# Merging one of four weight blocks partly on TensorE, and reordering the two-layer expert block around it

## The chip, the cores and the metric

One core of one Trainium2 chip runs the whole kernel. The metric is device time in microseconds for one execution, as the median of several runs. Besides these, one execution was recorded by the hardware profiler; its trace gives the start and the length of every instruction on every engine: TensorE (PE in the profile; its weight loads are PEld), VectorE (DVE), ScalarE (ACT), GpSimd (POOL) and SyncE's transfer queue (SP).

## The reference

The program is one layer of a graph network on 1250 nodes with 512 features: a two-step graph convolution, a linear-attention mixer, and at the end a feed-forward block whose weights are mixed at run time out of eight experts. The change touches only that last block:

```python
gh  = relu(x @ gfc1_w.T + gfc1_b)
g   = (gh @ gfc2_w.T + gfc2_b).mean(over the nodes)   # eight gates
W1m = W1 + sum_e g[e] * tv_W1[e]                      # 256 x 512
b1m = b1 + g @ tv_b1
W2m = W2 + sum_e g[e] * tv_W2[e]                      # 512 x 256
b2m = b2 + g @ tv_b2
h   = relu(x @ W1m.T + b1m)
out = h @ W2m.T + b2m
y   = layernorm(x + out) * ln_g' + ln_b'
```

The gates are means over all nodes, so no merged weight exists before the whole gating layer is done. Here `x` is the layer-normed input of the block; the result is added to the residual stream. All data are float32.

## The kernel before

**Layout.** A tile is 128 nodes: ten node tiles (`NT`), the last with 98 rows. Features lie in `DT = 4` blocks of 128. The first layer has 256 outputs, `FT = 2` blocks of 128. `xn2_t` holds the normed input with the features on the partitions; `CHUNKS` cuts its 1250 columns into three pieces (418, 416, 416), so that one piece fits a PSUM bank.

**Order.** From the last graph convolution on, every engine's order is the order in which the Python code issues the instructions (`last_order`, a manual schedule); semaphores are put in wherever data, or the reuse of a buffer, ask for it. The eight PSUM banks are handed out at first use, the one that came free longest ago first.

**The stretch in question**, from L1274 to the end of `usual_block`:

1. `gate_products` (L1278, L1281) computes the eight gates, once as a row on every partition (`pg`) and once as a column (`pg9`). DVE turns the first into `gate` (L1297), ACT the second into `gate9` (L1298).
2. The merged first-layer weights `m1` have four feature blocks of 128 x 256, and each is summed over eight experts in one of two ways. On DVE: a chain of `scalar_tensor_tensor` into a PSUM accumulator (`merge`, L1312), and at its end, unless `alone`, an addition of the base weights (L1315). On ACT and POOL: ACT scales the expert's block in place (`scaled`, L1307) and POOL adds it to `m1` (L1347 for block 3, L1320 in `merge_far`). Before the change DVE sums block 0 (`alone`), then 1, then 2, and ACT with POOL sums block 3.
3. The second-layer weights `m2` have two halves of 128 x 512: ACT with POOL sum half 1 (`merge_far`), DVE sums half 0.
4. `joined(c)` (L1325) multiplies block `c` of `m1` with block `c` of the input into six open PSUM banks (`parts`: two output blocks by three pieces). After `c = 3` ACT writes `a_t` with bias and ReLU (L1328).
5. The merged second bias comes from one product with `gate9` (L1334); ACT copies it to `b2` (L1342) and back to PSUM (L1358). It is added to the normed input of tiles 0 to 4 by DVE (L1364) and of tiles 5 to 9 by POOL (L1366).
6. The output loop: `out_product(t)` (L1374) are two products over 512 columns; `out_sum` (L1378) and `out_gauge` (L586, L588, L590) follow on DVE and ACT. Then tiles 2, 5 and 9 are finished by DVE (`out_near`, L1392 to L1395) and the other seven by ACT and POOL (`out_far`, L1402 to L1408; two POOL operations, L1406 and L1407).

The matrix unit takes one float32 product of this program as two LDWEIGHTS and two MATMUL instructions: the 24 products of `joined` are 48 rows in the profile.

Of the kernel before, what the change touches and what calls it, by code (L numbers as in the profile page):

```python
# [9 lines left out]
F32 = mybir.dt.float32  # L10
# [3 lines left out]
AF = mybir.ActivationFunctionType  # L14
ALU = mybir.AluOpType
AX = mybir.AxisListType

P = 128
N = 1250
D = 512  # L20
DT = D // P
NT = 10
FF = 256
FT = FF // P
NE = 8
# [16 lines left out]
CHUNKS = [(0, 418), (418, 416), (834, 416)]  # L42


def rows(t):
    return min(P, N - t * P)
# [479 lines left out]
def usual_block(  # L526
# [23 lines left out]
    nc = tc.nc  # L550
# [3 lines left out]
    tmp = ctx.enter_context(tc.tile_pool(name="tmp", bufs=2))  # L554
# [7 lines left out]
    def bank(dtype=F32):  # L562
        return psum.tile([P, 512], dtype, tag="bank", name="bank")
# [14 lines left out]
    ident = const.tile([P, P], F32, name="ident")  # L578
# [49 lines left out]
    def v(name, i=0, n=1):  # L628
        at = _COLS[name][0] + i
        return v_sb[:, at:at + n]  # L630
# [43 lines left out]
    g2bc = const.tile([NE, 1], F32, name="g2bc")  # L674
# [108 lines left out]
    key = e_d  # L783
# [333 lines left out]
    late = ctx.enter_context(tc.tile_pool(name="late", bufs=1, side="right"))  # L1117
    r9 = late.tile([NE + 1, 3, D], F32, name="r9")
    nc.sync.dma_start(out=r9, in_=rows9)
    m1 = late.tile([P, DT, FF], F32, name="m1")  # L1120
    nc.sync.dma_start(out=m1, in_=f_w1.rearrange("(c p) f -> p c f", p=P))
    m2 = late.tile([P, FT, D], F32, name="m2")
    nc.sync.dma_start(out=m2, in_=f_w2.rearrange("(c p) f -> p c f", p=P))
    t1s, t2s = [], []
# [11 lines left out]
    gate9 = late.tile([NE + 1, P], F32, name="gate9")  # L1136
# [137 lines left out]
    pg, pg9 = bank(), bank()  # L1274
# [20 lines left out]
    gate_products([DT - 1])  # L1295
    gate = late.tile([P, NE], F32, name="gate")
    nc.vector.scalar_tensor_tensor(gate, pg[:, 0:NE], 1.0 / N, v("g2b", 0, NE), op0=ALU.mult, op1=ALU.add)  # L1297
    nc.scalar.activation(gate9[0:NE, :], pg9[0:NE, 0:P], AF.Identity, bias=g2bc, scale=1.0 / N)  # L1298

    a_t = more.tile([P, FT, N], F32, tag="E", name="a_t")
    parts = [(f, b, bank()) for f in range(FT) for b in range(len(CHUNKS))]
    sums = [bank(), bank()]

    def scaled(dst, e, src):
        nc.scalar.activation(dst, src, AF.Copy, scale=gate[:, e:e + 1])  # L1307

    def merge(acc, dst, srcs, at, alone=False):

        for e in range(0 if alone else 1, NE):
            nc.vector.scalar_tensor_tensor(dst[at] if alone and e == NE - 1 else acc, srcs[e][at], gate[:, e:e + 1],  # L1312
                                           dst[at] if alone and e == 0 else acc, op0=ALU.mult, op1=ALU.add)
        if not alone:
            nc.vector.tensor_tensor(dst[at], acc, dst[at], ALU.add)  # L1315

    def merge_far(dst, srcs, at):
        for e in range(NE):
            scaled(srcs[e][at], e, srcs[e][at])
            nc.gpsimd.tensor_tensor(dst[at], dst[at], srcs[e][at], ALU.add)  # L1320

    def joined(c):
        for f, b, ps in parts:
            c0, cn = CHUNKS[b]
            nc.tensor.matmul(ps[:, :cn], m1[:, c, f * P:(f + 1) * P], xn2_t[:, c, c0:c0 + cn],  # L1325
                             start=(c == 0), stop=(c == DT - 1))
            if c == DT - 1:
                nc.scalar.activation(a_t[:, f, c0:c0 + cn], ps[:, :cn], AF.Relu, bias=mb1[:, f:f + 1])  # L1328

    def first(c):  # L1330
        return (slice(None), c, slice(None))


    nc.tensor.matmul(sums[1], gate9, r9[:, 0, :], start=True, stop=True)  # L1334
    b2 = late.tile([P, D], F32, name="b2")
    merge(sums[0][:, 0:FF], m1, t1s, first(0), alone=True)
    mb = late.tile([P, FT, NE], F32, name="mb")
    nc.gpsimd.tensor_tensor(mb, v("tvb1", 0, FT * NE).rearrange("p (f e) -> p f e", f=FT),
                            gate.unsqueeze(1).to_broadcast([P, FT, NE]), ALU.mult)
    mb1 = late.tile([P, FT], F32, name="mb1")  # L1340
    scaled(t1s[0][first(3)], 0, t1s[0][first(3)])
    nc.scalar.copy(b2, sums[1])  # L1342
    scaled(sums[1][:, 0:FF], 0, t1s[0][first(1)])
    for e in range(NE):
        if e:
            scaled(t1s[e][first(3)], e, t1s[e][first(3)])
        nc.gpsimd.tensor_tensor(m1[first(3)], m1[first(3)], t1s[e][first(3)], ALU.add)  # L1347
    joined(0)
    scaled(sums[0][:, 0:FF], 0, t1s[0][first(2)])
    merge(sums[1][:, 0:FF], m1, t1s, first(1))  # L1350
    joined(1)
    merge_far(m2, t2s, first(1))
    scaled(sums[1], 0, t2s[0][first(0)])
    merge(sums[0][:, 0:FF], m1, t1s, first(2))
    joined(2)
    nc.vector.tensor_reduce(mb1, mb, AX.X, ALU.add)
    nc.gpsimd.tensor_tensor(mb1, mb1, v("fb1", 0, FT), ALU.add)
    nc.scalar.copy(sums[0], b2)  # L1358
    merge(sums[1], m2, t2s, first(0))
    joined(3)  # L1360
    for t in range(NT):
        n = rows(t)
        if t < NT // 2:
            nc.vector.tensor_tensor(xn2[0:n, t, :], xn2[0:n, t, :], sums[0][:n], ALU.add)  # L1364
        else:
            nc.gpsimd.tensor_tensor(xn2[0:n, t, :], xn2[0:n, t, :], b2[:n], ALU.add)  # L1366

    last = {}

    def out_product(t):  # L1370
        n = rows(t)
        last[t] = bank()
        for f in range(FT):
            nc.tensor.matmul(last[t][:n], a_t[:, f, t * P:t * P + n], m2[:, f, :], start=(f == 0), stop=(f == FT - 1))  # L1374

    def out_sum(t):
        n = rows(t)
        nc.vector.tensor_tensor(last[t][:n], last[t][:n], xn2[0:n, t, :], ALU.add)  # L1378

    def out_gauge(t):  # L1380
        last[t] = (last[t],) + spread(last[t][:rows(t)], rows(t))
# [26 lines left out]
        nc.sync.dma_start(out=out[t * P:t * P + n, :], in_=m[:n])  # L1408

    for t in range(NT + 1):  # L1410
        if t < NT:
            out_product(t)
            out_sum(t)
        if t >= 1:
            (out_near if t - 1 in (2, 5, 9) else out_far)(t - 1)
        if t < NT:
            out_gauge(t)
# [5 lines left out]
def graph_block(tc, *args):  # L1423

    unusual = usual_block(tc, *args)
    with tc.If(unusual > 0):
        general_block(tc, *args)
# [58 lines left out]
```

## Time and profile before

| What | us |
|---|---|
| Median of three runs (574.11 to 574.74) | 574.61 |
| The profiled execution, its own time | 574.88 |
| Its span, from the first to the last instruction | 572.9 |
| Busy PE / DVE / ACT / POOL in the span | 546.3 / 324.8 / 242.0 / 80.1 |
| `gate` done (L1297, start 517.44) | 517.61 |
| First product of `joined` starts (L1325) | 521.91 |
| First `out_product` starts (L1374) | 541.42 |
| First POOL operation of the output loop (L1406) | 547.16 |
| Last POOL operation starts (L1407) | 565.97 |

How to read it: times within the trace count from the start of the span. The execution's own time is 1.98 us more than its span. A row of a view gives a start, a length, an engine, a source line and the tile names "out<-in"; "idle before" is how long the engine had stood still and who released it. PEclk is the TensorE clock that was granted in a stretch, as a share of full speed.

### The profile page before, as it was taken

What the parts mean: (1) busy time and instruction counts of PE and PEld (TensorE: products, weight loads), DVE (VectorE), ACT (ScalarE), POOL (GpSimd) and SP (SyncE); (2) the same over time, 40 slices, a digit from 0 to 9 for tenths busy, and PEclk for the clock granted to TensorE, in tenths of its full rate; (3) what the DMA queues carried; (4) which work ended last, traced back from release to release, by engine and by line L of the source; (5) the groups of instructions that cost most, each with busy time, mean ns of one, the idle gap of its engine ahead of it and who ended that gap; (6) DMA issues with size and microseconds to landing.
All of it is one profiled execution on the core that took longest, in us unless ns stands there. A gap on an engine that the chain in (4) does not pass through costs nothing.

```text
span 572.9 us, 6957 instructions
## 1 busy us (share of the span) xinstructions
PE 546.3 (95%) x2367; PEld 369.1 (64%) x2367; DVE 324.8 (57%) x1097; ACT 242.0 (42%) x533; POOL 80.1 (14%) x77
## 2 busy tenths in 40 slices
PE   8799999999999999999999999999999999997990
PEld 7665568799955477777854454459995557764540
DVE  4579999976899734444425534111113248708693
ACT  5676664454444112322333443113323456727242
POOL 7200000000000000000013331000000001106975
PEclk9899999999999999999999999999999999997995
DMA  9400200020030020000311002000009120402023
GB/s 287 176 1 1 74 2 1 1 74 2 1 113 36 0 74 0 1 1 1 111 37 52 22 1 73 0 0 1 2 0 348 55 74 1 146 1 75 0 76 110
DMA packets 19285, 29.10 MB, mean 51 GB/s; under 512 B 1529, under 2 KB 8185, under 8 KB 19240
## 3 DMA queue, kind: packets, MB, share of 16 engines
q1 hardware_dynamic: 18984, 28.32, 14.6%
q8 instruction: 20, 0.33, 0.2%
q10 hardware_dynamic: 256, 0.25, 0.2%
q14 instruction: 25, 0.20, 0.1%
HBM read 26.01 MB, written 2.56 MB: 50 GB/s over the span
## 4 chain that ended last, share of the span: by engine, by line
PE 87%; DVE 5%; ACT 3%; POOL 2%; issue 1%; DMA 1%; POOLq 0%; DVEq 0%; ACTq 0%
PE bank L576 28%; PE bank L981 16%; PE bank L968 12%; PE bank L917 6%; PE bank L1037 6%; PE bank L849 5%; PE bank L1064 5%; PE bank L1325 3%; PE bank L606 2%; PE bank L1374 1%; POOL m L1406 1%; POOL m L1407 1%; DVE st L586 1%; PE bank L902 1%; ACT xn L600 1%
## 5 line engine op out<-in xcount | busy, mean ns | idle before, releaser
L981 PE MATMUL bank<-adj,y_h 128*128 128x416 f32 (+1 forms) x240 | 86.5, 361 | 1.1 <-DVE adj L851 1.1
L981 PE MATMUL bank<-adj,y_l 128*128 128x416 f32 (+1 forms) x240 | 84.4, 352 | 0.0
L834 DVE TENSOR_SCALAR oh_k<-count,e_d 128x240 f16<-128x240 f16 x324 | 82.6, 274 | 0.0
L1083 POOL TENSOR_TENSOR m<-m,ls_bc 128x512 f32<-128x512 f32 (+1 forms) x10 | 12.7, 1269 | 447.3 <-ACT m L600 447.3
L968 PE MATMUL bank<-w,h_t 128*128 128x512 f32 (+1 forms) x160 | 70.4, 592 | 0.0
L576 PE MATMUL bank<-z_t,w 128*128 128x416 f32 (+1 forms) x192 | 68.9, 513 | 0.0
L576 PEld LDWEIGHTS bank<-z_t,w 128*128 128x128 f32 x192 | 36.1, 189 | 31.8 <-issue 29.9
L832 DVE TENSOR_SCALAR oh_s<-count,s_lo 128x128 f16<-128x128 f16 x220 | 54.1, 246 | 0.0
L968 PEld LDWEIGHTS bank<-w,h_t 128*128 128x128 f32 (+1 forms) x160 | 29.4, 188 | 34.8 <-issue 34.5
L614 DVE SCALAR_TENSOR_TENSOR z_t<-u,m_sb,z_t 128x416 f32<-128x416 f32 (+1 forms) x24 | 15.7, 653 | 59.8 <-ACT u L613 59.8
L981 PEld LDWEIGHTS bank<-adj,y_h 128*128 128x128 f32 x240 | 45.1, 188 | 2.6 <-issue 2.1
L981 PEld LDWEIGHTS bank<-adj,y_l 128*128 128x128 f32 x240 | 45.2, 188 | 1.2 <-issue 0.7
L849 PE MATMUL bank<-oh_k,oh_s 128*128 128x240 f16 x324 | 41.4, 266 | 1.4 <-ACT oh_s L818 1.2
L849 PEld LDWEIGHTS <-oh_s 128*128 128x128 f16 x324 | 31.6, 98 | 15.8 <-issue 5.1
L612 ACT ACTIVATE z_t<-bank,v_sb 128x416 f32<-128x416 f32 (+1 forms) x24 | 14.6, 608 | 61.5 <-PE bank L981 61.5
L851 DVE TENSOR_TENSOR adj<-adj,bank 128x240 f32 x81 | 32.3, 399 | 13.9 <-PE bank L849 12.5
L995 DVE BATCH_NORM_STATS2 bst<-bank 128x6 f32<-128x416 f32 (+1 forms) x24 | 14.4, 600 | 42.9 <-ACT h_t L994 42.9
L917 PE MATMUL bank<-kk,xn 128*128 128x128 f32 (+1 forms) x320 | 38.4, 275 | 0.0
L576 PE MATMUL bank<-xn_t,lw 128*128 128x256 f32 (+2 forms) x128 | 37.6, 439 | 0.3 <-ACT xn_t L607 0.3
L917 PEld LDWEIGHTS bank<-kk,xn 128*128 128x128 f32 (+1 forms) x320 | 37.0, 192 | 0.1
L1064 PE MATMUL bank<-mixer,q_t 128*128 128x512 f32 (+1 forms) x80 | 36.3, 592 | 0.0
L576 PE MATMUL bank<-xn_t,gw 128*128 128x256 f32 (+2 forms) x128 | 35.3, 427 | 0.9 <-ACT xn_t L607 0.9
(166 smaller groups left out, 800.0 us busy)
## 6 DMA issues: line engine op xcount, KB each, us to landing
t<-in_tv_w SPq DMA_DIRECT2D x12, 512.0 KB, 7.5
w<-in_conv_w SPq DMA_DIRECT2D x4, 1024.0 KB, 5.5
x_in<-in_x SPq DMA_DIRECT2D x9, 256.0 KB, 4.6
xt<-in_x SPq DMA_DIRECT2D x9, 256.0 KB, 4.1
out<-m SPq DMA_DIRECT2D x9, 256.0 KB, 2.4
rest<-in_tv_w SPq DMA_DIRECT2D x4, 512.0 KB, 4.8
lw<-in_lin_w SPq DMA_DIRECT2D x4, 256.0 KB, 4.9
wk<-in_w_qkv SPq DMA_DIRECT2D x1, 1024.0 KB, 7.0
```

What stands on the lines that cost most here:

```text
L576: nc.tensor.matmul(ps[:, :cn], lhs(c), rhs(c), start=(c == 0), stop=(c == k - 1))
L614: nc.vector.scalar_tensor_tensor(dst, u[:, :cn], minus(*slope), dst, op0=ALU.mult, op1=ALU.add)
L832: nc.vector.tensor_scalar(oh_s[:, j, :], count16[:, 0:P], s_lo[:, b, j:j + 1], None, op0=ALU.is_equal)
L834: nc.vector.tensor_scalar(oh_k[:, j, :], count16, key[:, b, j:j + 1], None, op0=ALU.is_equal)
L849: nc.tensor.matmul(ps[:, 0:NT * W], oh_s[:, j, :], oh_k[:, j, :], start=(j == 0), stop=(j == J - 1))
L851: nc.vector.tensor_tensor(adj_r[:, :, at], adj[:, :, at], ps[:, 0:NT * W].rearrange("p (s d) -> p s d", s=NT), ALU.add)
L917: nc.tensor.matmul(ps[:, c * P:(c + 1) * P], xn[0:n, t, c * P:(c + 1) * P], k_nodes(f)[0:n, t, :], start=(t == 0), stop=(t == NT - 1))
L968: nc.tensor.matmul(ps[:n], h_t[:, c, t * P:t * P + n], w1[:, c, :], start=(c == 0), stop=(c == DT - 1))
L981: nc.tensor.matmul(ps[:, :cn], y[0:n, s, f * P:(f + 1) * P], adj_r[0:n, s, c0:c0 + cn], start=(s == 0 and y is ys[0]), stop=(s == NT - 1 a ...
L1037: nc.tensor.matmul(ps[:n], xn_t[:, c, t * P:t * P + n], wq[:, c, :], start=(c == 0), stop=(c == DT - 1))
L1064: nc.tensor.matmul(ps[:n], q_t[:, h, t * P:t * P + n], mixer[:, h, :], start=(h == 0), stop=(h == DT - 1))
L1325: nc.tensor.matmul(ps[:, :cn], m1[:, c, f * P:(f + 1) * P], xn2_t[:, c, c0:c0 + cn], start=(c == 0), stop=(c == DT - 1))
```

## The change

Block 0 of `m1` is cut in two column halves. The left half (columns 0 to 127, output block `f = 0`) is summed by TensorE: eight 128 x 128 identities, each scaled by one gate (`gated`; four made by DVE, four by ACT), and a plain identity for the base weights are multiplied with the weights into one PSUM bank, and ACT copies the sum into `m1`. The right half stays on DVE. Block 1 moves from DVE to ACT and POOL. Blocks 2 and 3 are summed together by DVE in one chain of 512 columns, in place of two chains of 256. The product for the second bias moves from ahead of `joined(0)` to behind it, into the bank of DVE's accumulator, so that the copy back to PSUM goes; the copy to `b2` then stands in ACT's order ahead of the scaling for `m2`. The scaling and adding for half 1 of `m2` is issued in two groups of four, with the start value of half 0 between them. `parts` is ordered by piece first, and the two products of `joined(3)` that belong to the last piece are issued behind two output tiles.

```diff
-    nc.scalar.activation(gate9[0:NE, :], pg9[0:NE, 0:P], AF.Identity, bias=g2bc, scale=1.0 / N)
-    parts = [(f, b, bank()) for f in range(FT) for b in range(len(CHUNKS))]
+    parts = [(f, b, bank()) for b in range(len(CHUNKS)) for f in range(FT)]
     sums = [bank(), bank()]
...
+    def flat(w, c0, c1):
+        return w[:, c0:c1, :].rearrange("p c f -> p (c f)")
...
+    def merge_far(dst, srcs, es):
+        for e in es:
+            scaled(srcs[e], e, srcs[e])
+            nc.gpsimd.tensor_tensor(dst, dst, srcs[e], ALU.add)
+    def joined(c, which):
+        for f, b, ps in which:
...
+    gated = [tmp.tile([P, 2, P], F32, tag="xt", bufs=4, name="gated") for _ in range(NE // 2)]
+    one = [flat(t, 1, 2) for t in t1s]
+    two = [flat(t, 2, 4) for t in t1s]
+    for e in (0, 1, 4, 5):
+        nc.vector.tensor_scalar(gated[e // 2][:, e % 2, :], ident, gate[:, e:e + 1], None, op0=ALU.mult)
+    scaled(gated[1][:, 0, :], 2, ident)
+    scaled(gated[1][:, 1, :], 3, ident)
+    nc.scalar.activation(gate9[0:NE, :], pg9[0:NE, 0:P], AF.Identity, bias=g2bc, scale=1.0 / N)
+    merge_far(flat(m1, 1, 2), one, [0])
+    scaled(gated[3][:, 0, :], 6, ident)
+    scaled(gated[3][:, 1, :], 7, ident)
+    nc.tensor.matmul(sums[1][:, 0:P], ident, m1[:, 0, 0:P], start=True, stop=False)
     for e in range(NE):
+        nc.tensor.matmul(sums[1][:, 0:P], gated[e // 2][:, e % 2, :], t1s[e][:, 0, 0:P],
+                         start=False, stop=(e == NE - 1))
+    acc = sums[0][:, 0:FF - P]
+    for e in range(NE):
+        nc.vector.scalar_tensor_tensor(m1[:, 0, P:FF] if e == NE - 1 else acc, t1s[e][:, 0, P:FF], gate[:, e:e + 1],
+                                       m1[:, 0, P:FF] if e == 0 else acc, op0=ALU.mult, op1=ALU.add)
+    merge_far(flat(m1, 1, 2), one, [1])
+    nc.scalar.copy(m1[:, 0, 0:P], sums[1][:, 0:P])
+    joined(0, sorted(parts, key=lambda p: p[0]))
+    merge_far(flat(m1, 1, 2), one, [2])
+    scaled(sums[1], 0, two[0])
+    merge_far(flat(m1, 1, 2), one, range(3, NE))
     nc.vector.tensor_reduce(mb1, mb, AX.X, ALU.add)
+    merge(sums[1], flat(m1, 2, 4), two)
     nc.gpsimd.tensor_tensor(mb1, mb1, v("fb1", 0, FT), ALU.add)
+    nc.tensor.matmul(sums[0], gate9, r9[:, 0, :], start=True, stop=True)
+    nc.scalar.copy(b2, sums[0])
...
+    far2 = [t[:, 1, :] for t in t2s]
+    joined(1, parts)
+    merge_far(m2[:, 1, :], far2, range(4))
+    shifted(0)
+    scaled(sums[1], 0, t2s[0][:, 0, :])
+    merge(sums[1], m2[:, 0, :], [t[:, 0, :] for t in t2s])
+    merge_far(m2[:, 1, :], far2, range(4, NE))
+    joined(2, parts)
+    joined(3, parts[0:4])
+    for t in range(1, NT):
+        shifted(t)
...
     for t in range(NT + 1):
+        if t == 2:
+            joined(3, parts[4:])
```

`shifted(t)` is the addition of item 5 for one tile, unchanged.

More of the change, by code (lines that the diff above doesn't have):

```diff
@@ L1307, in scaled, with merge @@
         nc.scalar.activation(dst, src, AF.Copy, scale=gate[:, e:e + 1])
[L1309 to L1323, printed above, removed]
+    def flat(w, c0, c1):
+        return w[:, c0:c1, :].rearrange("p c f -> p (c f)")
+    def merge(acc, dst, srcs):
+        for e in range(1, NE):
+            nc.vector.scalar_tensor_tensor(acc, srcs[e], gate[:, e:e + 1], acc, op0=ALU.mult, op1=ALU.add)
+        nc.vector.tensor_tensor(dst, acc, dst, ALU.add)
+    def merge_far(dst, srcs, es):
[4 more added lines that the diff above has]
+        for f, b, ps in which:
             c0, cn = CHUNKS[b]
@@ L1328, in joined @@
                 nc.scalar.activation(a_t[:, f, c0:c0 + cn], ps[:, :cn], AF.Relu, bias=mb1[:, f:f + 1])
[L1330 to L1336, printed above, removed]
     mb = late.tile([P, FT, NE], F32, name="mb")
@@ L1340, in usual_block @@
     mb1 = late.tile([P, FT], F32, name="mb1")
-    scaled(t1s[0][first(3)], 0, t1s[0][first(3)])
-    nc.scalar.copy(b2, sums[1])
-    scaled(sums[1][:, 0:FF], 0, t1s[0][first(1)])
-    for e in range(NE):
[L1345 to L1352, printed above, removed]
@@ L1353, in usual_block @@
-    scaled(sums[1], 0, t2s[0][first(0)])
-    merge(sums[0][:, 0:FF], m1, t1s, first(2))
-    joined(2)
+    b2 = late.tile([P, D], F32, name="b2")
+    gated = [tmp.tile([P, 2, P], F32, tag="xt", bufs=4, name="gated") for _ in range(NE // 2)]
[4 more added lines that the diff above has]
+    scaled(gated[1][:, 0, :], 2, ident)
@@ L1356, in usual_block, with shifted @@
     nc.vector.tensor_reduce(mb1, mb, AX.X, ALU.add)
+    merge(sums[1], flat(m1, 2, 4), two)
     nc.gpsimd.tensor_tensor(mb1, mb1, v("fb1", 0, FT), ALU.add)
[L1358 to L1361, printed above, removed]
+    nc.tensor.matmul(sums[0], gate9, r9[:, 0, :], start=True, stop=True)
+    nc.scalar.copy(b2, sums[0])
+    def shifted(t):
         n = rows(t)
```

## The prediction

> **What bounds the kernel now.** I read the chain of waits first, since the change touches only the last 55 us:
>
> ```profile
> 517.44 0.18 DVE gate L1297
> ...
> 517.64 0.56 DVE bank L1312
> ...
> 521.37 0.49 DVE m L1312
> 521.86 0.04 issue
> 521.91 19.68 PE bank L1325 x48
> 541.59 6.88 PE bank L1374 x16
> ...
> 553.44 1.28 POOL m L1406
> ...
> 566.43 0.80 POOL m L1407
> ```
>
> After the gates the end waits for DVE's eight steps on block 0 (4.2 us), then TensorE without a break up to the fourth output tile, then the output loop on DVE, ACT and POOL. Only what comes before the output loop, or makes TensorE quicker, can move the end.
>
> Second, windows of 3.41 us, with PE's busy time as the first number after the length and PEclk behind the five engines:
>
> ```profile
> 22.03:25.44 3.41, 0.97 (x6) 0.68 (x5) 2.19 (x8) 1.43 (x4) 0.00 (x0) 1.00 0.00 0
> 25.44:28.86 3.42, 3.42 (x12) 2.74 (x11) 1.60 (x6) 2.52 (x7) 0.00 (x0) 0.50 0.00 0
> ...
> 45.92:49.34 3.42, 2.22 (x14) 1.37 (x12) 3.42 (x18) 2.80 (x7) 0.00 (x0) 1.00 0.00 0
> 49.34:52.75 3.41, 3.41 (x15) 2.22 (x15) 3.17 (x15) 1.86 (x5) 0.00 (x0) 1.00 0.00 0
> ...
> 516.96:520.38 3.42, 1.87 (x8) 0.69 (x6) 2.73 (x7) 1.78 (x5) 0.94 (x2) 1.00 0.85 304
> 520.38:523.79 3.41, 1.88 (x3) 1.17 (x4) 3.23 (x7) 3.41 (x10) 2.58 (x4) 0.50 0.02 5
> 523.79:527.21 3.42, 3.42 (x6) 1.61 (x6) 3.21 (x8) 3.42 (x6) 3.19 (x5) 0.50 0.00 0
> ```
>
> Windows with 0.97, 1.87 and 1.88 us of PE work are followed by one at half clock; the one with 2.22 is not. So the wait for block 0 costs twice: TensorE stands still, and then runs at half clock until 527.2. The weight loads of L1325 stand 0.35 us apart at full clock and 0.70 before: 48 x 0.352 = 16.9, measured 19.7, so 2.8 us are lost.
>
> Third, the timeline of POOL, for what else must be ready:
>
> ```profile
> 526.50 2.62 POOL L1320 TENSOR_TENSOR m<-m,t 128x512 f32<-128x512 f32 x2
> 537.32 6.18 POOL L1366 TENSOR_TENSOR xn<-xn,b 128x512 f32<-128x512 f32 x5
> 547.16 1.26 POOL L1406 TENSOR_TENSOR m<-m,ln_g 128x512 f32<-128x512 f32 x1 [3.67 <-ACT m L600]
> ```
>
> Half 1 of `m2` takes POOL 10.7 us (526.50 to 537.20, 1.34 an addition), the five tiles 6.2; then POOL waits 3.7 us. Last, the groups that give prices:
>
> ```profile
> L917 PE MATMUL bank<-kk,xn 128*128 128x128 f32 (+1 forms) x320 | 38.4, 275 | 0.0
> L1312 DVE SCALAR_TENSOR_TENSOR bank<-t,gate,bank 128x256 f32<-128x256 f32 x20 | 9.8, 489 | 0.6
> L1307 ACT ACTIVATE t<-t,gate 128x256 f32<-128x256 f32 x8 | 3.4, 493 | 0.0
> L1347 POOL TENSOR_TENSOR m<-m,t 128x256 f32<-128x256 f32 x8 | 5.8, 728 | 2.8 <-ACT t L1307 2.4
> ```
>
> **The change part by part.** Times are on the axis of this trace; `gate` is done at 517.61.
>
> *Eight gated identities.* A DVE `tensor_scalar` of 128 f32 columns is not in the trace. Nearest: L785, 328 ns for 324 f32 columns, and L832, 246 ns for 128 f16 columns, started 0.17 apart. I take 0.23 and 0.15 apart (bounds 0.17 and 0.39 apart): DVE has its four by 518.3. ACT, from 493 ns (256 columns) and 708 (512): 0.385 each, 0.31 apart. ACT's order is identities 2 and 3, `gate9`, the first scaling of block 1, identities 6 and 7: done at 518.0, 518.35, 518.65, 519.05, 519.35, 519.66.
>
> *Nine narrow products.* They go into a bank long free (banks go out at first use, oldest free first), so the plain identity needs nothing and runs at 517.6. L917, which also accumulates with new weights each time, gives 0.12 an instruction, 0.24 a product. Isolated, the last pair of L1278 took 0.39 (517.01 to its end); that is the upper bound of a link. Back to back, seven products end at 519.4; the last two wait for ACT: 519.4 and 519.7; the sum is there at 520.2, ACT's copy (0.36, as L1298) at 520.6. `joined(0)` starts at 520.7 on the left half: **1.2 us earlier**. The right half costs DVE eight steps of 0.385 from 518.3 (128 columns, between 167 ns for 8 in L1297 and 489 for 256): 521.4, before its first product at 522.8. Experts 6 and 7 are read by TensorE from 519.4; SP issued those transfers before 466. No transfer is moved; the last pair (issued 515.78) has landed by 520 and is read after 529.
>
> [...]
>
> *The clock.* In 516.96 to 520.38 PE now has the gate products and some 2.4 us of chain, over 2.2 in sum, so it should stay at full speed: **2.8 us won**. [...] The four executions known lie between 574.11 and 574.88, so I keep the trace's 2.8.
>
> *Bias product behind `joined(0)`.* Before it ran in TensorE's idle time; now it is on the path: 2 x 0.433 = **0.87 lost**. `joined(0)` is done at 520.7 + 6 x 0.704 = 524.9, the product at 525.8.
>
> *Block 1 on ACT and POOL.* The first two additions end at 520.85. Behind ACT's copy (which waits for the chain) stand the third scaling, DVE's start value and the rest; from the fourth POOL adds without a break, 522.0 + 5 x 0.745 = 525.7. `joined(1)` needs it at 525.8: **nothing, without any slack**. A microsecond of delay on POOL is one on TensorE.
>
> *Blocks 2 and 3 on DVE.* Start value at 521.5, seven steps of 0.78 and one of 0.7: 527.8. `joined(2)` needs it at 530.0: nothing.
>
> *The copy to `b2` ahead of the scaling for `m2`.* ACT waits for the bias product until 526.0; behind it stand the eight scalings, so POOL begins half 1 at 527.35 instead of 526.50: 8 x 1.34 = 10.7, done at 538.05. `joined(3)` without its last pair ends at 525.8 + 16 x 0.704 = 537.05, the first product of tile 0 at 537.9; its second waits until 538.1: **0.15 lost**. DVE's half 0 is ready at 535.9 (ACT gives its start value at 529.7, behind four scalings), the tiles' additions at 538.3: covered by `out_sum(0)` at 539.1. Gone is the copy back to PSUM (0.59 of ACT, idle anyway).
>
> *Two products behind two tiles.* Tiles 0 and 1 come 1.4 us earlier than they would; tile 2 ends at the same TensorE work: 538.97 + 1.73 + 1.41 + 1.73 = 543.85. DVE sums tile 2 at 544.0; before, 546.77: 2.8 earlier. From there both loops are alike: DVE sets tile 3, for which POOL waited at 553.44. POOL's own work allows it: half 1 at 538.05, five tiles 544.3, tiles 0 and 1 by 549.5, tile 3 at 550.6. ACT's two `a_t` operations (1.3) stand ahead of tile 1's normalisation and move it to 545.9; POOL takes tile 1 at 546.9.
>
> *Sum:* -1.2 - 2.8 + 0.87 + 0.15 = -3.0; laid out with the waits, -2.8. 574.88 - 2.8 = 572.1; the median lies 0.27 below the profiled execution, which would give 571.8. I say **572.0**.
>
> **The rivals.**
>
> *One window at half clock (G).* If the chain counts for less than its busy time, the window from 520.38 is at half: 1.6 us lost, **573.6**. For: short products with waits between. Against: 2.22 us was enough at 45.92.
>
> *Two windows, as before (N).* Then `joined(0)` and the bias product end near 529, POOL starts half 1 at 530, and 3.3 of the gain are gone: **575.3**. This is also the case that the change doesn't do what it says. Against: from 520.7 TensorE has work, so 520.38 to 523.79 is busy.
>
> *The sum goes link by link (S), slower.* If each link waits for its own weights at 0.45, the sum ends at 521.6, `joined(0)` starts at 522.05, and PE's window is as empty as before: half clock until 527.2. The bias product ends at 529.7, `b2` at 530.5, half 1 of `m2` at 541.95; tile 2 is summed at 547.9 against 546.77: +1.1, **576.0**. The change loses from the point where the copy to `b2` ends after 529.45 (forecast 526.6), because the pair behind the tiles and the late `m2` then add. For: `gated` comes from two engines in turn. Against: six of eight identities are ready before their turn.
>
> **How the numbers follow.** Forecast 0.60 (its own range 571.2 to 572.9), G 0.14, N 0.13, S 0.09, a larger gain 0.04 (POOL's gap at tile 3 also shrinks). About 0.2%, or 1.15 us, is what a measurement of this kernel can tell from no change: faster is below 573.46, slower above 575.76. Faster: 0.60 + 0.04 + nearly half of G = 0.70. Within: the rest of G and most of N = 0.18. Slower: S and a tail of N = 0.12. The range 571.0 to 574.6 leaves out S, most of N and half of the larger gain.
>
> **What the profile of the changed kernel would show.** Right: PEclk 1.00 from 517 to 540; first L1325-like product near 520.7; bias product near 525; first addition of half 1 on POOL near 527.3; sum of tile 2 near 544.0; last POOL operation 2.8 earlier. Wrong: half clock after 520.4; a wait of TensorE at `joined(1)` or at tile 0's second product over 0.3; POOL's first L1406 after 545; a new wait ahead of tile 3.

## The result, and the profile after

The changed kernel took **572.30 us** (median of seven runs, 572.17 to 572.92). The kernel before, on the same chip and in turn with it, took 574.17 us (seven runs, 573.59 to 575.25). The ratio is 0.9965, with a 95% interval of 0.9954 to 0.9976: 0.35% faster, and the forecast was 572.0. The profiled execution of the changed kernel took 572.41 us, with a span of 570.5; that of before took 574.88, with a span of 572.9. So the traces differ by 2.4 to 2.5 us, the medians by 1.9.

The chain of waits after, from the gate products on (start, length, what):

```profile
517.59 0.42 PE bank L1346 x2
518.00 2.05 PE bank L1348 x16
520.08 0.27 ACT m L1355
520.35 0.41 ACT t L1306
...
525.46 0.73 POOL m L1320
526.19 0.04 issue
526.23 11.46 PE bank L1325 x32
537.70 3.43 PE bank L1392 x8
541.13 1.40 PE bank L1325 x4
542.53 3.45 PE bank L1392 x8
...
550.96 1.28 POOL m L1424
...
563.96 0.80 POOL m L1425
```

DVE's eight steps (L1312 before) are gone from the chain. TensorE's own sum stands in their place: L1346 is the product with the plain identity, L1348 the eight with gated ones. The source lines are those of the changed kernel (L1392 is `out_product`, L1424 and L1425 are POOL's two operations of the output loop). But `joined(0)` and the product for the second bias are not on this chain either: it runs from the copy L1355 through ACT's scalings and POOL's additions for block 1, and comes back to TensorE only at `joined(1)`, at 526.23.

The windows after (length, busy PE, PEld, DVE, ACT, POOL with counts, then PEclk, the DMA share and GB/s):

```profile
516.96:520.38 3.42, 3.08 (x22) 2.56 (x22) 2.86 (x11) 2.63 (x9) 1.30 (x3) 1.00 0.81 296
520.38:523.79 3.41, 3.39 (x10) 1.94 (x11) 3.24 (x7) 2.99 (x7) 2.55 (x4) 1.00 0.01 5
523.79:527.21 3.42, 3.11 (x9) 1.20 (x8) 3.27 (x5) 1.25 (x3) 2.33 (x4) 1.00 0.00 0
```

PE's 1.87 us in the first window have become 3.08, and the two windows behind it, granted at half before, are at full clock. TensorE's timeline (start, length, then the instructions; in brackets the idle time before them and who ended it):

```profile
517.91 2.14 PE L1348 MATMUL bank<-t,gated 128*128 128x128 f32 x16
520.40 4.47 PE L1325 MATMUL bank<-xn_t,m 128*128 128x418 f32 x12 [0.36 <-ACT m L1355]
524.80 1.12 PE L1364 MATMUL bank<-r,gate 9*128 9x512 f32 x2
526.23 11.46 PE L1325 MATMUL bank<-xn_t,m 128*128 128x418 f32 x32 [0.31 <-POOL m L1320]
537.53 3.60 PE L1392 MATMUL bank<-m,a_t 128*128 128x512 f32 x8
```

The chain of eight gated products ran without a break in 2.14 us. Besides the 0.36 us for ACT's copy there is one new wait: 0.31 us at `joined(1)`, for POOL's last addition to block 1.

The stretch before the gates shifts by up to 0.8 us from one profile to another (`gate` starts between 517.04 and 517.86), so I count from the start of `gate` in each profile. "Summed" marks the start of DVE's sum for the tile (`out_sum`), and "end" is the end of POOL's last operation. Each row is one execution.

| us after the start of `gate` | `joined(0)` starts | tile 0 summed | tile 2 summed | first POOL operation of the output loop | end |
|---|---|---|---|---|---|
| before | 4.47 | 25.90 | 29.33 | 29.72 | 49.79 |
| after | 3.09 | 22.14 | 26.97 | 26.78 | 47.44 |

In this count `joined(0)` starts 1.38 earlier, tile 2 is summed 2.36 earlier and the end comes 2.35 earlier. What is won is there by tile 2 and is handed on unchanged.

### The profile page after: what moved, and what is told of

Its sections match the earlier page's. It is cut to its first block, busy times and chain, and to the rows that moved or that the text cites. A ratio compares the mean times of both kernels' runs of the same rounds, so it can differ in the third digit from the quotient of the medians.

```text
span 570.5 us, 7005 instructions
## 1 busy us (share of the span) xinstructions
PE 546.5 (96%) x2385; PEld 370.3 (65%) x2385; DVE 322.9 (57%) x1093; ACT 243.0 (43%) x536; POOL 80.1 (14%) x77
## 4 chain that ended last, share of the span: by engine, by line
PE 87%; DVE 4%; ACT 4%; POOL 3%; issue 1%; DMA 1%; POOLq 0%; DVEq 0%; ACTq 0%
PE bank L576 28%; PE bank L981 16%; PE bank L968 12%; PE bank L917 6%; PE bank L1037 6%; PE bank L849 5%; PE bank L1064 5%; PE bank L1325 2%; PE bank L606 2%; PE bank L1392 1%; POOL m L1424 1%; POOL m L1425 1%; DVE st L586 1%; PE bank L902 1%; ACT xn L600 1%
## 5 line engine op out<-in xcount | busy, mean ns | idle before, releaser
L834 DVE TENSOR_SCALAR oh_k<-count,e_d 128x240 f16<-128x240 f16 x324 | 83.8, 279 | 0.0
L832 DVE TENSOR_SCALAR oh_s<-count,s_lo 128x128 f16<-128x128 f16 x220 | 55.3, 251 | 0.0
```

Of the source, the lines that this page charges most:

```text
L832: nc.vector.tensor_scalar(oh_s[:, j, :], count16[:, 0:P], s_lo[:, b, j:j + 1], None, op0=ALU.is_equal)
L834: nc.vector.tensor_scalar(oh_k[:, j, :], count16, key[:, b, j:j + 1], None, op0=ALU.is_equal)
```

## The experiments

My theory: most of the gain is the clock, which TensorE's own sum keeps at full speed; the earlier start adds a smaller part; block 1 on POOL takes some of it back. The rivals: that the earlier start is what counts and the clock little; that the bias product behind `joined(0)` is what takes the gain back; that the pair behind two tiles carries a part of it. The twelve kernels ran in three groups; each has the kernel before beside it on its own chip. A diff is against the changed kernel unless it says "before".

### The changed kernel again

No edit, twice: `after_again` in the first group, `after_third` in the last.

> The changed kernel once more, as the measure for the three others on this chip. Every theory: 572.3 us (572.0 to 572.8), 1.9 us under the kernel before, with no window at half clock between 517 and 540 us.

> The changed kernel once more, as the measure for the three others on this chip. Every theory: 572.3 to 572.7 us.

Measured: 572.68 us (ratio 0.9973, 0.9961 to 0.9985) and 572.60 (0.9968, 0.9956 to 0.9980). Counted from `gate`, `joined(0)` starts at 3.08 in both, tile 2 is summed at 26.98 and 26.97, and the end is at 47.44 and 47.43. So in a kernel that keeps its clock a difference of 0.05 us at one of these marks can be read from one profile, while the runs of before spread over one to two microseconds. The verdicts below rest on the marks, and the times stand beside them. The marks of before are those of one execution with two windows at half clock; what its other runs say is told further down.

### Before, with the clock kept up

```diff
(before)
+    for _ in range(3):
+        nc.tensor.matmul(parts[0][2], ident, xn2_t[:, 0, 0:512], start=True, stop=True)
     merge(sums[0][:, 0:FF], m1, t1s, first(0), alone=True)
```

Three products whose result is thrown away fill TensorE's wait behind the bias product.

> The kernel before, unchanged but for three products over 512 columns that TensorE does while it waits for block 0; their result goes into a bank that the first product of joined overwrites, so nothing is computed differently. Theory (the gain is the clock): joined starts at 521.9 as before but at full clock, its 24 products take 17.0 instead of 19.7 us, tile 2 is summed near 544.1 instead of 546.8, and the time is that of the changed kernel, 572.2 us, within 0.4. Rival 1 (the earlier start counts for itself): 1.2 us above the changed kernel, 573.5. Rival 2 (products without a use don't hold the clock, or it falls for another reason): 574.2, as before.

Measured: 572.98 us (ratio 0.998, 0.9959 to 1.0001); end at 48.78, which is 1.01 before that of before. The expected full clock didn't come in the profiled execution. The windows:

```profile
516.56:519.98 3.42, 2.97 (x15) 1.53 (x15) 2.13 (x6) 1.35 (x5) 0.94 (x2) 1.00 0.79 270
519.98:523.39 3.41, 3.41 (x5) 1.35 (x4) 3.20 (x8) 3.38 (x9) 1.83 (x3) 0.50 0.12 44
```

A window with 2.97 us of busy PE is followed by one at half clock. That breaks the reading of the prediction, in which 2.22 us were enough. PE's timeline shows what the 2.97 consist of:

```profile
517.75 0.39 PE L1281 MATMUL bank<-gm,v_sb 128*8 128x128 f32 x2
518.59 1.12 PE L1334 MATMUL bank<-r,gate 9*128 9x512 f32 x2 [0.45 <-ACT gate L1298]
519.64 4.54 PE L1336 MATMUL bank<-xn_t,ident 128*128 128x512 f32 x6
```

Gate products that give 8 columns or 8 rows, a wait, and a bias product that reads 9 rows, fill it up to 519.64; only 0.34 us are of products of full size. The three fillers then ran at half clock (4.54 us, where four instructions take 1.99 at full clock below) and held `joined(0)` back to 6.16 after `gate`. So this trace doesn't tell the clock's worth.

Its six runs fall apart: three took 571.90 to 572.21 us with a granted clock of 0.989 to 0.990, three, the profiled one (574.25) among them, 573.75 to 575.65 with 0.984 to 0.985. The first three fit the theory (572.2, within 0.4), and they lie below all six runs of the changed kernel on the same chip (572.47 to 573.07). So where these useless products do keep the clock, the kernel before may be as quick as the changed one. None of the three has a trace, and why the next kernel, on another chip, doesn't come as low is not known.

The fillers were then placed better.

```diff
(before)
+    nc.tensor.matmul(parts[0][2], ident, xn2_t[:, 0, 0:512], start=True, stop=True)
     nc.tensor.matmul(sums[1], gate9, r9[:, 0, :], start=True, stop=True)
+    for _ in range(2):
+        nc.tensor.matmul(parts[0][2], ident, xn2_t[:, 0, 0:512], start=True, stop=True)
+    for _ in range(2):
+        nc.tensor.matmul(parts[0][2][:, 0:P], ident, xn2_t[:, 0, 0:P], start=True, stop=True)
```

> The kernel before with products that have no use, better placed: one over 512 columns ahead of the bias product, where TensorE waits for gate9, and two over 512 and two over 128 behind it. In the first try the window from 516.56 to 519.98 still counted as idle although PE was busy for 2.97 us of it; gate products (8 columns or 8 rows) and the bias product (9 rows) made up most of that. Theory (only work that fills the array counts, and the gain is the clock): with 0.87 us more of full work early in the gap no window is idle, joined starts near 522.0 at full clock, and the time is that of the changed kernel or up to 0.3 above, 572.3 to 572.9, without the runs of 574 and 575 of the first try. Rival 1 (the early start and the new order count for themselves): 573.5. Rival 2 (the clock falls all the same): 573.5 to 575, spread over two levels.

Measured: 573.09 us (ratio 0.9979, 0.9971 to 0.9988), which lies between the theory's 572.3 to 572.9 and the 573.5 of the rival that the early start and the new order count for themselves. All twelve runs have a granted clock of 0.988 to 0.991. Windows, and then TensorE's and ACT's timeline:

```profile
516.37:519.78 3.41, 3.41 (x15) 1.38 (x13) 2.43 (x7) 0.80 (x4) 0.94 (x2) 1.00 0.85 308
519.78:523.19 3.41, 3.41 (x12) 1.94 (x13) 3.23 (x7) 3.38 (x9) 1.62 (x3) 1.00 0.01 4
```

```profile
519.65 1.99 PE L1337 MATMUL bank<-xn_t,ident 128*128 128x512 f32 x4
...
521.91 16.97 PE L1325 MATMUL bank<-xn_t,m 128*128 128x418 f32 x48
538.72 1.02 PE L1379 MATMUL bank<-m,a_t 128*128 128x512 f32 x2
540.10 5.39 PE L1379 MATMUL bank<-m,a_t 128*128 128x512 f32 x12 [0.36 <-ACT a_t L1328]
```

```profile
537.85 3.10 ACT L1328 ACTIVATE a_t<-bank,mb 128x418 f32<-128x418 f32 x6 [7.46 <-POOL mb L1362]
```

The 48 instructions of `joined` take 16.97 us, where they took 19.68: with the clock alone kept up and nothing of the change's order, 2.7 us are won there. At the end 1.99 are left (47.80 against 49.79), mainly because `out_product(0)` now waits for `a_t`: ACT's bias for it is made on POOL behind half 1 of `m2`. In the changed kernel POOL makes it ahead of half 1 (L1362, at 526.14), and this wait is not there. **By the marks, 1.99 of the change's 2.35 us can be had by the clock alone.** By the medians on this chip it is less, 1.09 (574.18 to 573.09) of 1.58 (`after_third`, 572.60): the profile of before is one of its slower runs.

### The change without TensorE's sum

```diff
... (shortened: the lines of the gated identities, the nine narrow products and ACT's copy into m1[:, 0, 0:P] are taken out)
-    acc = sums[0][:, 0:FF - P]
+    acc = sums[0][:, 0:FF]
     for e in range(NE):
-        nc.vector.scalar_tensor_tensor(m1[:, 0, P:FF] if e == NE - 1 else acc, t1s[e][:, 0, P:FF], ...
+        nc.vector.scalar_tensor_tensor(m1[:, 0, :] if e == NE - 1 else acc, t1s[e][:, 0, :], ...
```

`block0_dve` is this; `block0_dve_filled` has four products of 512 columns and two of 128 ahead of the loop besides, with results that nothing reads.

> The changed kernel with block 0 summed by DVE alone again (eight steps of 256 columns; no gated identities, no narrow products, no copy into m1). Theory: TensorE stands still from 517.5 to 521.8, the clock is at half for up to two windows, joined(0) and the bias product end near 529.5 instead of 525.8, the copy to b2 and with it half 1 of m2 come 3.5 us later, and the time is 574.6 to 575.7 us: no better than the kernel before. Rival (the clock is not tied to the narrow products): only the start is lost, 573.0 to 573.5.

> The same with TensorE kept busy while DVE sums block 0: four products over 512 columns and two over 128 into a bank that is overwritten later. It separates the clock from the earlier start. Forecast's sum (the start counts in full): 1.3 us above the changed kernel, 573.6. Theory now (in the changed kernel joined(1) waits for block 1 from ACT and POOL anyway, until 526.2): joined(0) from 521.8 and the bias product end at 526.9, joined(1) starts there, and only 0.7 us are lost: 573.0.

Measured: `block0_dve` 575.78 us (ratio 1.0022, 1.0015 to 1.0030), **slower than before**; `block0_dve_filled` 573.55 (0.9990, 0.9983 to 0.9997). TensorE's timeline and a window of the first, and the same products of the second:

```profile
522.08 6.45 PE L1325 MATMUL bank<-xn_t,m 128*128 128x418 f32 x12 [4.24 <-ACT t L1306]
528.46 1.12 PE L1352 MATMUL bank<-r,gate 9*128 9x512 f32 x2
529.51 11.46 PE L1325 MATMUL bank<-xn_t,m 128*128 128x418 f32 x32
```

```profile
519.40:522.81 3.41, 0.73 (x1) 0.50 (x2) 3.23 (x8) 2.63 (x7) 3.02 (x6) 0.50 0.21 82
```

```profile
521.72 4.47 PE L1325 MATMUL bank<-xn_t,m 128*128 128x418 f32 x12
526.13 1.12 PE L1356 MATMUL bank<-r,gate 9*128 9x512 f32 x2
527.18 11.46 PE L1325 MATMUL bank<-xn_t,m 128*128 128x418 f32 x32
```

`joined(0)` takes 6.45 against 4.47, and the ends are 50.56 and 48.58: 1.98 in both places, which is the clock's share once more, now inside the change. By the medians it is 2.23 (575.78 to 573.55). The filled one starts `joined(0)` at 4.47, like before, and ends 1.14 after the changed kernel (0.87 by the medians, `after_again` 572.68): that is what the earlier start of 1.38 is worth. Expected were 1.3 by the forecast's sum and 0.7 by my theory; the measured 1.14 and 0.87 lie between. My 0.7 took `joined(0)` and the bias product together at 5.1 us again; the rows give 5.46 (521.72 to 527.18). (`block0_dve`'s idle time of 4.24 is put down to ACT by the trace; the work it waits for is DVE's sum of block 0.)

`block0_dve` has the same gap as before and also two windows at half clock, and yet ends 0.77 later. These windows lie differently over the products (to 526.1, in before to 527.2), so the pair at full clock is the better measure: `block0_dve_filled` ends 0.78 after `before_filled_2` (48.58 and 47.80). So the reordering without the narrow products is a loss. What in it costs is argued: TensorE goes straight from the bias product to `joined(1)`, and `joined(1)` starts 5.46 after `joined(0)`, where in `before_filled_2`, with the bias product ahead, it is 4.21. No run moves the bias product alone there.

The three steps add up to the whole: from 49.79 to 47.80 by the clock, to 48.58 by the reordering, to 47.44 by the earlier start that TensorE's own sum brings.

### The bias product, and block 1

```diff
-    nc.tensor.matmul(sums[0], gate9, r9[:, 0, :], start=True, stop=True)
+    nc.scalar.copy(sums[0], ln_b)
```

This leaves the experts' share out of the second bias.

> The changed kernel without the product for the merged second bias: ACT copies ln_b into its bank instead, so the output has a wrong bias; all other work is as it was. It asks what the product's new place behind joined(0) costs. Forecast's step: 0.87 us on the path, so 571.4 us. Theory now: joined(1) waits for block 1 (ACT and POOL) until 526.2 in any case, so TensorE only stands idle from 525.0 to 526.2, and the time stays at 572.3, within 0.2; POOL begins half 1 of m2 a microsecond earlier and that is worth nothing.

Measured: 572.40 us (ratio 0.9967, 0.9955 to 0.9979); `joined(1)` starts 8.93 after `gate` (after: 8.92), tile 2 is summed at 26.97 (26.97), the end is at 47.43 (47.44). TensorE waits in the place of the product:

```profile
525.97 11.47 PE L1325 MATMUL bank<-xn_t,m 128*128 128x418 f32 x32 [1.37 <-POOL m L1320]
```

So in the changed kernel the bias product costs nothing: it fills 1.06 us of a wait for POOL that would be 1.37 without it.

```diff
-    merge_far(flat(m1, 1, 2), one, [2])
+    merge_far(flat(m1, 1, 2), one, [2, 3])
     scaled(sums[1], 0, two[0])
-    merge_far(flat(m1, 1, 2), one, range(3, NE))
+    merge_far(flat(m1, 1, 2), one, range(4, NE))
```

> The changed kernel with two ACT operations exchanged: the scaling of block 1's fourth expert ahead of the start value for DVE's chain of 512 columns. In the changed kernel POOL waits 0.63 us for that scaling. Theory now (block 1 sets joined(1)): the wait goes, block 1 is ready at 525.6 and joined(1) starts at 525.7, when the bias product is done; 0.5 us won, 571.8. DVE's chain starts 0.3 later, which nobody waits for. Forecast's step (block 1 isn't late): no change, 572.3.

Measured: 571.96 us (ratio 0.9958, 0.9944 to 0.9971). POOL's timeline of the changed kernel, and then POOL's and TensorE's of this one:

```profile
520.03 1.58 POOL L1320 TENSOR_TENSOR m<-m,t 128x256 f32<-128x256 f32 x2 [0.31 <-ACT t L1306]
522.24 3.94 POOL L1320 TENSOR_TENSOR m<-m,t 128x256 f32<-128x256 f32 x5 [0.63 <-ACT t L1306]
```

```profile
520.33 5.60 POOL L1320 TENSOR_TENSOR m<-m,t 128x256 f32<-128x256 f32 x7 [0.31 <-ACT t L1306]
```

```profile
526.15 11.47 PE L1325 MATMUL bank<-xn_t,m 128*128 128x418 f32 x32
537.45 3.72 PE L1392 MATMUL bank<-m,a_t 128*128 128x512 f32 x8
```

ACT's third and fourth scalings now come ahead of DVE's start value, and POOL's gap of 0.63 is closed. The wait at `joined(1)` is gone, and it starts at 8.54 after `gate` (8.92), 0.38 sooner, where I had expected 0.5. At the end 0.26 are left (47.18): the products of the first output tiles take 3.72 us, not 3.60, since half 1 of `m2` is no earlier (POOL's first operation of the output loop: 26.75 and 26.78), as the next run confirms.

```diff
     (as block1_sooner, and:)
+    far2 = [t[:, 1, :] for t in t2s]
+    merge_far(m2[:, 1, :], far2, range(2))
     nc.scalar.copy(b2, sums[0])
...
     joined(1, parts)
-    merge_far(m2[:, 1, :], far2, range(4))
+    merge_far(m2[:, 1, :], far2, range(2, 4))
```

ACT's first two scalings for `m2` no longer stand behind its wait for the bias product.

> The changed kernel with the two ACT operations of block1_sooner exchanged and, in addition, the first two scalings for half 1 of m2 ahead of the copy to b2. In block1_sooner joined(1) started 0.4 us earlier but the second product of tile 0 then waited 0.1 for half 1 of m2. Theory: POOL goes from block 1 to half 1 without a break, half 1 is ready 1.4 us earlier, the wait is gone, and 0.4 us are won against the changed kernel. Rival (half 1 was never late, the tail takes it back): no more than block1_sooner, 0.2.

Measured: 572.46 us, 0.14 below `after_third` on the same chip; these times can't tell the two apart. By the marks POOL's first operation of the output loop comes 1.3 us sooner (25.52), tile 2 0.38 (26.59), the end 0.38 (47.06). So the 0.12 that `block1_sooner` lost at the first tiles is back, and the rest of POOL's lead brings nothing.

### The pair of first-layer products

```diff
-    joined(3, parts[0:4])
+    joined(3, parts)
...
-        if t == 2:
-            joined(3, parts[4:])
```

> The changed kernel with all six products of joined(3) ahead of the output loop, as before the change. Forecast and theory: TensorE's work ahead of tile 2 is the same in both orders, tile 2 sets the rest, so 572.3 us within 0.2, although tiles 0 and 1 are summed 1.4 us later and POOL stands idle before its first L1424. Rival (POOL needs the early start of tiles 0 and 1): slower by up to 1 us, 573.3.

Measured: 572.37 us (ratio 0.9965, 0.9953 to 0.9977). Tile 0 is summed at 23.52 (22.14), tile 2 at 26.95 (26.97), the end is at 47.41 (47.44). Two tiles come 1.4 us later, and nothing is lost: the end hangs on tile 3, which is behind the pair either way. The pair behind two tiles is no part of the gain.

```diff
-        if t == 2:
+        if t == 4:
```

> The changed kernel with the two products of joined(3) behind four output tiles instead of two (tile 6 is the first that needs them). Theory: tile 2 and tile 3 are summed 1.4 us earlier, DVE goes through the loop without a break from tile 3 on, TensorE is ahead of it by then and takes the two products for nothing: 1.2 us won, 571.1. Rival (POOL is already full: its first L1424 at 544.1 follows the tiles' bias additions directly): 0.3 won, 572.0. A second rival (ACT writes a_t too late for tile 6): slower.

Measured: 571.65 us (ratio 0.9955, 0.9941 to 0.9969). Tile 3 is summed at 27.28 (28.69), 1.4 sooner, and the end is at 46.67, 0.77 sooner, not the 1.2 expected. POOL's timeline at tile 3, in this kernel and in the changed one:

```profile
550.40 1.27 POOL L1424 TENSOR_TENSOR m<-m,ln_g 128x512 f32<-128x512 f32 x1 [1.00 <-ACT m L600]
```

```profile
550.96 1.27 POOL L1424 TENSOR_TENSOR m<-m,ln_g 128x512 f32<-128x512 f32 x1 [1.70 <-ACT m L600]
```

POOL still waits 1.00 us for the normalised tile 3. ACT's two `a_t` operations for the late pair now stand in its queue between tile 3's sum and tile 3's normalisation, and the chain of waits of this run goes through them.

### All three together

`two_sooner`, and the pair placed by hand at `t == 3`: on TensorE behind four tiles, on ACT ahead of tile 3's square root.

```diff
     (as two_sooner, without the pair at t == 2, and:)
         if t >= 1:
             (out_near if t - 1 in (2, 5, 9) else out_far)(t - 1)
+        if t == 3:
+            joined(3, parts[4:])
         if t < NT:
             out_gauge(t)
```

> Both of these, and the last two products of joined(3) behind four tiles, with their ACT operations ahead of the square root of tile 3, where ACT is idle, instead of ahead of tile 3's normalisation. Theory: 0.4 from the front and 1.2 to 1.4 from tiles 2 and 3 summed earlier: 1.6 us under the changed kernel, 570.8. Rival (POOL's first L1424, behind the tiles' bias additions, becomes the bound): 1.0 under it, 571.4.

Measured: **571.26 us** (ratio to before 0.9943, 0.9929 to 0.9957), 1.34 below the changed kernel on the same chip (572.60). The end is at 46.27, 1.17 before the changed kernel's, which is what `two_sooner` (0.38) and `behind_four` (0.77) give together (1.15); the place on ACT's queue brought next to nothing. The time is nearer to the rival's 571.4 than to the 570.8 expected, but not for the rival's reason: POOL's first operation of the loop waits 0.19 for ACT. POOL's timeline, and then the chain of waits:

```profile
542.97 1.27 POOL L1425 TENSOR_TENSOR m<-m,ln_g 128x512 f32<-128x512 f32 x1 [0.19 <-ACT m L600]
...
549.52 1.26 POOL L1425 TENSOR_TENSOR m<-m,ln_g 128x512 f32<-128x512 f32 x1 [1.35 <-ACT m L600]
...
556.00 1.26 POOL L1425 TENSOR_TENSOR m<-m,ln_g 128x512 f32<-128x512 f32 x1 [1.29 <-ACT m L600]
```

```profile
545.73 3.45 PE bank L1393 x8
...
549.27 0.70 DVE bank L1397
...
555.14 0.79 ACT m L600
...
556.00 1.26 POOL m L1425
```

POOL waits 1.35 us for tile 3, but the end no longer hangs on it. The chain leads from TensorE's products of tiles 4 and 5, which stand behind the late pair, through DVE's work on tiles 5 to 7 to tile 6, for which POOL waits again, 1.29 us.

## Why the prediction was right, and where its steps were off

**The narrow products: right, a little pessimistic.** Forecast was `joined(0)` at 3.26 after `gate` (520.7); measured 3.09. The eight gated products took 2.14 / 8 = 0.27 each (forecast 0.24 back to back) without the break of 0.3 that I had put ahead of the last two; ACT's copy took 0.27, not 0.36. The prices of the identities, which no row of before showed, by groups:

```profile
L1306 ACT ACTIVATE gated<-ident,gate 128x128 f32<-128x128 f32 x4 | 1.4, 392 | 1.2 <-DVE gate L1297 1.2
L1339 DVE TENSOR_SCALAR gated<-ident,gate 128x128 f32<-128x128 f32 x4 | 0.9, 291 | 0.0
```

ACT's were right (385 ns forecast, 392 measured); DVE's were low (230 against 291), and hidden. DVE's first identity, beside which POOL's L1331 (0.22) ran, took 344 ns and the other three 273 to 274. No run shows the 0.1 that the forecast has between the end of ACT's copy (520.6) and `joined(0)` (520.7); the trace after has 0.05 there (520.35 and 520.40). Rival S, 0.45 a link, falls with the 0.27.

**The clock: right in outcome, wrong in its reason.** PEclk is 1.00 in every window from 517 to the end of TensorE's work, so rivals G and N did not happen; the 2.8 us are 2.7 at the products (`before_filled_2`) and 1.98 to 1.99 at the end (both pairs of experiments). But "2.2 us of busy PE are enough" is not a rule: in `before_filled` 2.97 were not. Had the change filled the gap with products as slim as the gate products, my argument would have promised the same full clock; that it came out is luck as far as this argument goes. Rival G's condition, that the chain counts for less than its busy time, fits better with `before_filled` (2.97 us, then a window at 0.50), but no run tests it by itself.

**Bias product, 0.87 lost, and block 1, "nothing, without any slack": these are the mis-sized terms, and block 1 hides the bias product.** By my working `joined(1)` would start at 525.8, 5.1 us after `joined(0)`; it took 5.83. TensorE alone needed 5.45 (`block1_sooner`, 520.70 to 526.15): `joined(0)` 4.40 and not 4.22, the bias product 1.05 and not 0.87. The other 0.38 is POOL: its five last additions began at 522.24, not 522.0, and stand 0.80 apart (five in 3.94), not 0.745, so block 1 was there at 526.19, not 525.7. Both prices could have been read before, in the rows of the bias product itself and of block 3's additions:

```profile
518.16 1.12 PE L1334 MATMUL bank<-r,gate 9*128 9x512 f32 x2 [0.45 <-ACT gate L1298]
520.98 5.57 POOL L1347 TENSOR_TENSOR m<-m,t 128x256 f32<-128x256 f32 x7 [1.67 <-ACT t L1307]
```

Seven additions in 5.57, each 0.73 long, stand 0.81 apart; my 0.745 is nearly the length of one. And I gave a path without slack no price: with no slack, each tenth late costs a tenth. Because POOL's path ends last, the bias product lies hidden under it and its removal is worth 0.00. A sign that I had named for being wrong, a wait of over 0.3 at `joined(1)`, came, with 0.31.

**Half 1 of `m2`: right.** It starts at 527.25 (forecast 527.35) and ends at 538.0 (538.05), in a trace whose `gate` starts 0.13 sooner. The wait of 0.15 at tile 0's second product did not come, since that product itself came later by what `joined(1)` lost.

**The pair behind two tiles, nothing at the end: right.** `not_behind` ends 0.03 us from the changed kernel.

**The sum.** Tile 2 was to be summed 2.8 sooner and was 2.36 sooner: 0.17 more at the start, 0.73 less up to `joined(1)`, and about 0.15 more at the first output tiles, from the wait that did not come. From there the loops are alike, as forecast (end 2.35 sooner).

**From the profile to the median.** I kept the trace's 2.8 for the gain against the median too. No run shows what would give the 572.9 at the upper end of the forecast's own range; what the runs show is that the time of before goes with its granted clock. Of the 68 runs of the kernel before in the three groups, 26 had a granted clock of 0.980 or 0.981 and a median of 574.77; 23 had 0.983 to 0.986 and 574.12; 19 had 0.987 to 0.989 and 573.66. `block0_dve`, which has the gap too, goes from 576.23 (nine runs, 0.982 to 0.983) to 574.91 (three, 0.988). The changed kernel's 19 runs all had 0.986 to 0.991, and there the clock sorts little (572.59 for the 13 up to 0.988, 572.38 for the rest). One window of 3.41 us at half (before, 520.38 to 523.79) lowers the mean clock of the whole run by 0.003, by my estimate from the trace (half of 3.41 in 572.9). So these figures fit that before has one such window more or less behind 520 from run to run, and that the profiled execution of 574.88, with two such windows, lies with the 26. It isn't shown: none of the 68 runs has a trace here, and another window, near 25 us, is at half too (25.45 to 28.86 before, 26.00 to 29.41 after). The two profiled executions are 2.47 apart, the medians 1.87: 0.6 less. The forecast of the time itself was off by the sum alone: 572.1 for the profiled execution, which took 572.41.

## What to carry to other kernels

A gap in TensorE's work can cost more behind the gap than in it (here 1.98 and 1.14 us): look at the granted clock in the windows after it, and price the half-clock stretch as its own term before pricing the wait. With products of full size, early in the gap, the clock stayed up here, even with ones whose result nobody reads (`before_filled_2`: 1.00 in both windows from 516.37 to 523.19; `block0_dve_filled`: 0.987 to 0.992 over the run in all 21 runs, against 0.982 to 0.988 in the 16 of `block0_dve`); with three that began late in it, at 519.64, it did not in the profiled execution (`before_filled`: 0.50 from 519.98 to 523.39). Useful ones won the start too (1.38 us, and 1.14 at the end). Where a forecast finds a path with no slack, take the distance of its steps from their starts and not from their lengths (here 0.81 and 0.73 us for POOL's additions), and expect that what runs beside it is worth nothing until that path is shortened (here the bias product, 0.00).

## What the runs showed of the hardware

**Busy time in the profile did not sort the windows by the clock that followed.** Behind a window with 2.97 us (`before_filled`; the expectation of `before_filled_2` calls it idle) the granted clock was 0.50, while behind one with 2.22 us (before, 45.92), the one with 3.08 (after) and the one with 3.41 from 516.37 (`before_filled_2`) it was 1.00. The 2.97 held 0.34 us of products of full size, the 3.41 of `before_filled_2` about 1.2 us of them. The theory in that expectation fits these four, but no run shows it: the size of the products was not varied alone, and the windows' places differ too. One more window asks for care: in before, 520.38 to 523.79 holds 1.88 us of `joined`, at half clock, and is followed by another at half. So 1.2 us of full-size products at full clock went with 1.00 behind them, and 1.88 us at half clock with 0.50.

**The granted clock can sort the runs of one kernel.** The median of the kernel before moves by 1.1 us between the upper and the lower group of its granted clocks, about 0.2% of its time; that of the changed kernel, which keeps its clock behind 520, by 0.2 us. Read the granted clock of a profiled execution against that of the other runs before its span is taken for typical.

**Tile 3.** In the changed kernel and in all its variants POOL waits 1.0 to 2.0 us for tile 3's normalisation by ACT. That is less room than it looks. In the changed kernel the chain of waits goes through tile 3 to tile 6, but DVE's path to tile 6 is ready with it: ACT has the scale of tile 6 at 556.09, and POOL is done with tile 4 at 556.15. A quicker tile 3 alone would win under 0.1 us there, by my estimate from these two times; no run tried it. Nor was it tried to keep the bias product ahead of `joined(0)` in `two_sooner`, where it would no longer be covered.
